# A convolution, Mamba and FFN network on one core: the FFN two steps later, and the scan's last column copied ahead of the product

## The chip, the cores and the metric

The kernel runs on one core of a Trainium2 chip. The metric is the device time of one execution in microseconds (us); the median of three runs before the change is 28348.76 us (28341.41 to 28352.17). A core has engines with queues of their own, each of which works strictly in order: TensorE (PE in the profile; PEld is its weight load), VectorE (DVE), ScalarE (ACT), GpSimd (POOL) and SyncE (SP, which here issues the DMAs). An instruction can wait for other engines through semaphores, and everything behind it on its engine waits too.

## The reference

Eight images of 64 channels and 128 x 128 pixels go through three parts: a front (a learned high-pass filter and norms), a bidirectional Mamba block of two layers, and a mix with an FFN. Cut to what the change touches:

```python
def selective_scan(u, dt, A, Bm, Cm, D, z):
    dt = jax.nn.softplus(dt)
    dA = jnp.exp(jnp.einsum('bdl,dn->bldn', dt, A))
    dBu = jnp.einsum('bdl,bnl,bdl->bldn', dt, Bm, u)
    ...
    _, hs = jax.lax.associative_scan(comb, (dA, dBu), axis=1)   # h = dA * h + dBu along l
    y = jnp.einsum('bldn,bnl->bdl', hs, Cm) + D[None, :, None] * u
    return y * jax.nn.silu(z)
...
g = conv2d(xn, ffn_in_w, pad=0)
g = conv2d(g, ffn_dw_w, groups=2 * HID, pad=1)
g1, g2 = jnp.split(g, 2, axis=1)
g = jax.nn.gelu(g1, approximate=False) * g2
return x + conv2d(g, ffn_out_w, pad=0)
```

A sequence has 16384 positions, 128 channels and 16 states per channel, and is scanned in both directions in each of the two layers.

## The kernel before

**The unit of work.** A sequence is cut into 16 chunks of T = 1024 positions. The 2048 pairs of channel and state are laid on 128 partitions in U = 16 rounds, so a chunk has 16 scan steps, an image has 4 x 16 chunks (1024 steps), and the eight images have 512 chunks and 8192 steps. All other work (front, mix and FFN of one image) is placed beside the Mamba steps of another.

**The order is written by hand.** `at(time, phase, fn)` puts a function into step `time`; within a step the phases run FEED, SCAN, MID, PROD, EXP, DECAY, REST. The functions are called in the order of (step, phase), and each engine's queue gets its instructions in that order. What an instruction waits for is worked out from the tiles that it reads and writes; two engines that touch the same PSUM bank are ordered one after the other, in the order of the program, reads against reads too.

**One scan step u** (class `Chunk`; `plan` places it with b as the chunk's first step):

- `drive` (L1216, GpSimd): for two steps at once `bu` = dt*u * B into SBUF, four buffers.
- `decay` (L1221, ScalarE, phase EXP of step b+u-2): `w` = exp(dt * A), 128 x 1024, into one of two PSUM tiles that take turns, so decay of u+2 writes over the tile of u.
- `scan` (L1231, VectorE, phase SCAN): h = w * h + bu, from the state column that the previous chunk left. If `on_pool(u)`, h goes to the SBUF tile `hs`; otherwise back into `w` in PSUM.
- `product` (L1257): h times C. On GpSimd one step later if `on_pool(u)`, otherwise on VectorE in phase PROD of the same step, from `w` into `hs`. `on_pool` is true for u = 0, 2, 6 modulo 8, but for the step after a gelu (`gelu_times`, L1052).
- `keep` (L1268, ScalarE): copies the last column of h, 128 x 1, into `state` for the next chunk. For a VectorE step its source is the PSUM tile `w`; it stands in phase PROD and, in the list of that phase, behind `product`.
- `collect` (L1271, TensorE): sums over the states into `y`.

On ScalarE's queue the copy of step u is followed by the decay of u+2 (EXP), then by what DECAY holds in that step (PSUM tiles copied out for conv, gate, dt, the norms and so on), then by REST.

**Functions with a table of their own.** ScalarE's exp and ln share one table; silu, softplus and gelu each load another and load the first back (`logs_and_exps`, L68). They stand in REST: `silu` at step 11 modulo 16 (silu of `xc`, in half of the chunks of the gate as well), `softplus` at step 2 modulo 16.

**The FFN** (class `Ffn`, images 0 to 6 beside the next image's Mamba; the last image's FFN runs alone at the end on another plan). Its 16 row blocks stand FFN_STEP = 24 steps apart, from step FFN_AT of the image. With a as a block's first step: windows loaded at a-4 and a-3, `conv` groups of four parts at a, a+6 and a+14, `first_out` at a+5, `gelus` at a+11 in REST, `rest_times` at a+13, `times` at a+19 and a+21, `load_x2` at a+16, `project` at a+21, `add` and `store` at a+23.

Of the kernel before, what the change touches and what calls it, by code (L numbers as in the profile page):

```python
# [36 lines left out]
FEED, SCAN, MID, PROD, EXP, DECAY, REST = range(7)  # L37

IMAGE = 4 * NT * U
FRONT_STEP, MIX_STEP, FFN_STEP = 24, 13, 24  # L40
FRONT_AT, MIX_AT, FFN_AT = 593, 990, 1202

SILU, SOFTPLUS, GELU = 11, 18, 11

# [11 lines left out]
def kernel(ctx: ExitStack, tc: tile.TileContext, a: dict, out: bass.AP):  # L56
# [6 lines left out]
    nc = tc.nc  # L63
# [124 lines left out]
    with tc.tile_pool(name="wspill", bufs=1) as fp, tc.tile_pool(name="wprep", bufs=2) as pp, \  # L188
            tc.tile_pool(name="wps", bufs=4, space=PSUM) as pps:
        with tc.manual_schedule():  # L190
# [161 lines left out]
            for l in range(DEPTH):  # L352
# [9 lines left out]
                for d in range(2):  # L362
                    cw, xdt, xbc, dtn, al, dp = dirs[2 * l + d]
                    taps = by_taps(inx2, cw, DI, KC)
                    for j in range(KC):
                        t = turned(taps[:, j, :], ident, P, DI)
                        at = j if d == 0 else KC - 1 - j
# [39 lines left out]
    def at(time, phase, fn, *args):  # L407
        steps.setdefault((time, phase), []).append((fn, args))
# [466 lines left out]
    class Ffn:  # L875
# [139 lines left out]
        def plan(self, a):  # L1015
            early = 12 if self.alone else 0
            at(a - 4 - early, REST, self.load, 0)
            at(a - 3 - early, REST, self.load, 1)

            if self.alone:  # L1020
                at(a - 6, REST, self.before_taps)
                at(a - 5, DECAY, self.before_taps_out)
                at(a - 5, REST, self.taps, 0)
                at(a - 2, REST, self.taps, 1)
                groups = ((0, 0, self.first_out, 2), (3, 1, self.times, 6))
                gelus, out = 3, 9
            else:
                groups = ((0, 0, self.first_out, 5), (6, 2, None, 0), (14, 1, self.times, 19))
                gelus, out = GELU, 21
            for t, g, end, to in groups:  # L1030
                for i in range(4):
                    at(a + t + (0 if self.alone else i), REST, self.conv, g, i)
                for h in range(2 if end else 0):
                    late = 0 if self.alone or end == self.first_out else 2 * h
                    at(a + to + late, MID if end == self.times else DECAY, end, h)
            at(a + gelus, REST, self.gelus)
            at(a + gelus + 2, MID, self.rest_times)
            at(a + out - 5, REST, self.load_x2)
            at(a + out, REST, self.project)
            at(a + out + 2, DECAY, self.add)  # L1040
            at(a + out + 2, REST, self.store)
# [18 lines left out]
    class Chunk:  # L1060
# [205 lines left out]
                nc.gpsimd.tensor_tensor(out[:, ::-1], hs[:, ::-1], c[:, ::-1], ALU.mult)  # L1266

        def keep(self, u):  # L1268
            nc.scalar.copy(self.column(u), self.last(self.hs.pop(u)))  # L1269

        def collect(self, k):  # L1271

# [72 lines left out]
        def plan(self):  # L1345
            b = self.t0 - 2 * U

            def feed(t, fn, *args):
                if self.beside_front:
                    at(t, FEED, fn, *args)  # L1350
                else:
                    at(t - 1, REST, fn, *args)

            at(b + (5 if self.i == NCH - 2 else 3), REST, self.load_hn)
            for h in range(2):
                feed(b + 7 + h, self.conv, h)
                at(b + 7 + h, DECAY, self.conv_out, h)
                if self.second:
                    feed(b + 9 + h, self.gate, h)
                    at(b + 9 + h, DECAY, self.gate_out, h)  # L1360
                feed(b + 14 + h, self.step, h)
                at(b + 14 + h, DECAY, self.step_out, h)
            at(b + SILU, REST, self.silu)
            at(b + SOFTPLUS, REST, self.softplus)
            if self.second:
                at(b + 13, REST, self.store_gate)
            b = self.t0
            feed(b - 16, self.bc)
            at(b - 16, DECAY, self.bc_out)
            at(b - 14, REST, self.store_bc)  # L1370
            at(b - 13, REST, self.store_dt)
            at(b - 11, FEED, self.dtx)
            at(b - 10, REST, self.store_du)
            j0 = self.pairs[0][0] // 2
            at(b - 10, REST, self.load_states, "bp", j0)
            at(b - 8, REST, self.load_channels, "dup", 0)
            at(b - 6, REST, self.load_channels, "dtp", 0)
            at(b - 5, REST, self.load_states, "bp", 1 - j0)
            at(b - 4, REST, self.load_states, "cp", j0)
            at(b - 3, REST, self.load_channels, "dup", 1)  # L1380
            at(b - 2, REST, self.load_channels, "dtp", 1)
            at(b - 1, REST, self.load_states, "cp", 1 - j0)
            for k in range(U // 2):
                at(b + 2 * k - 5, REST, self.drive, k)
                at(b + 2 * k + 3 + (k % 4 == 0), REST, self.collect, k)
            for u in range(U):
                at(b + u - 2, EXP, self.decay, u)
                at(b + u, SCAN, self.scan, u)
                at(b + u + self.on_pool(u), FEED if self.on_pool(u) else PROD, self.product, u)
            for u in range(U):  # L1390
                at(b + u + self.on_pool(u), EXP if self.on_pool(u) else PROD, self.keep, u)
            for h in range(2):
                if self.second:
                    at(b + 8 * h + 1, REST, self.load_yf, h)
                    at(b + 8 * h + 6, REST, self.add_yf)
                    at(b + 8 * h + 7, REST, self.load_gate, h)
                if self.second:
                    at(b + 8 * h + 11, MID, self.y_out, h)
                else:
                    at(b + 8 * h + 10, DECAY, self.y_out, h)  # L1400
                    at(b + 8 * h + 11, REST, self.store_y, h)
            if not self.second:
                return
            b += U
            n = self.norm
            at(b + 2, REST, self.load_h)
            feed(b + 5, self.project)
            at(b + 6, DECAY, self.residual)
            at(b + 6, DECAY, self.square)
            if self.l == 0:  # L1410
                at(b + 7, REST, self.store_h)
            feed(b + 12, lambda: n.means(mm_tile, self.sq))
            at(b + 13, DECAY, n.means_out)
            feed(b + 17, n.spread, mm_tile)
            at(b + 19, MID, self.normed)
            if self.l:
                at(b + 20, DECAY, self.weighted)
            at(b + 20, REST, self.store_hn)
# [10 lines left out]
    for b in range(B):  # L1429
        a, last = IMAGE * b, b == B - 1  # L1430
# [36 lines left out]
```

## Time and profile before

The profiled execution took 28355.4 us and its span is 28353.5 us, so 1.9 us lie around the span.

| engine | busy us | share of the span | instructions |
|---|---|---|---|
| VectorE | 26988.0 | 95% | 17438 |
| GpSimd | 26586.1 | 94% | 7980 |
| TensorE (matmul) | 23008.2 | 81% | 98188 |
| ScalarE | 18798.4 | 66% | 29139 |

The mean granted TensorE clock is 0.883 of full speed. In image 2 the stretch beside the FFN (7886 to 9178 us) takes 1292 us for 388 steps, the one beside the front (9187 to 10649 us) 1462 us for 424 steps, and the one beside the mix (10640 to 11330 us) 690 us for 208 steps. Read a row of the profile's groups as line, engine, operation, what is written from what, count, busy time and mean of one in ns, and then the idle time of the engine just ahead of these instructions with what ended most of it.

### The profile page before, as it was taken

The page shows a single profiled execution, that of the slowest core. Times are in us where ns is not written, and L with a number is a line of the kernel's source. Part 1 is how long each engine was busy: PE and PEld are TensorE (multiplying, and loading weights), DVE is VectorE, ACT ScalarE, POOL GpSimd, SP SyncE. Part 2 cuts the span into 40 slices and gives each one's busy share as a digit, 9 for nine tenths or more (in the row PEclk, how much of TensorE's full clock was granted, in tenths as well). Part 3 has the DMA queues.
Part 4 walks back from the last instruction along what each step waited for, and adds up shares of the span by engine and source line. Part 5 has one row for each costly group of instructions (what it writes and reads, how often), then busy time and mean ns, then how long its engine had stood idle before and what let it go on. Part 6 is the DMA issues. An engine that isn't in the chain of part 4 may idle for free. (4 is left out here: it accounts for less than half of the span.)

```text
span 28353.5 us, 311709 instructions
## 1 busy us (share of the span) xinstructions
PE 23008.2 (81%) x98188; PEld 7334.6 (26%) x98188; DVE 26988.0 (95%) x17438; ACT 18798.4 (66%) x29139; POOL 26586.1 (94%) x7980
## 2 busy tenths in 40 slices
PE   7666888878888788887888888887888878888679
PEld 3212322223222232222322223222222222222113
DVE  6999999999999999999999999999999999999997
ACT  4666666666666666666666666666666666666663
POOL 4999999999999999999999999999999999999994
PEclk7777889988899888988889888998888988899789
DMA  6777787777877678777787777777777777777675
GB/s 161 232 242 228 236 261 249 248 228 240 264 245 250 226 237 270 242 248 229 244 261 247 240 231 248 258 248 240 234 250 251 250 237 234 255 254 251 216 250 155
DMA packets 2611073, 6796.34 MB, mean 240 GB/s; under 512 B 433558, under 2 KB 739110, under 8 KB 2608390
## 3 DMA queue, kind: packets, MB, share of 16 engines
q1 hardware_dynamic: 2608534, 6776.25, 73.7%
q8 instruction: 776, 12.71, 0.2%
q14 instruction: 883, 7.23, 0.1%
q10 hardware_dynamic: 880, 0.14, 0.0%
HBM read 5543.05 MB, written 1265.19 MB: 240 GB/s over the span
## 5 line engine op out<-in xcount | busy, mean ns | idle before, releaser
L1218 POOL TENSOR_TENSOR bu<-dup,bp 128x2048 f32<-128x2048 f32 x4096 | 18594.4, 4548 | 52.2 <-DMA dup<-du_dram 26.1
L1226 ACT ACTIVATE w<-dtp,a_neg 128x1024 f32<-128x1024 f32 x8192 | 9163.6, 1119 | 1429.0 <-DVE hs L1247 601.6
L1262 DVE TENSOR_TENSOR hs<-w,cp 128x1024 f32<-128x1024 f32 x5232 | 6391.1, 1222 | 199.0 <-DMA cp<-bc_dram 46.6
L1247 DVE TENSOR_TENSOR_SCAN w<-w,state,bu 128x1024 f32<-128x1024 f32 x2651 | 6210.2, 2343 | 88.6 <-ACT w L1226 58.7
L1245 DVE TENSOR_TENSOR_SCAN w<-w,state,bu 128x1024 f32<-128x1024 f32 x2581 | 6048.2, 2343 | 121.8 <-ACT w L1226 105.0
L1284 PE MATMUL y<-hs,sel_y 128*32 128x512 f32 x32768 | 4944.7, 681 | 569.3 <-POOL hs L1266 445.5
L1269 ACT COPY state<-w 128x1 f32<-128x1 f32 x5232 | 828.0, 158 | 5178.4 <-DVE hs L1262 5119.6
L1264 POOL TENSOR_TENSOR hs<-hs,cp 128x1024 f32<-128x1024 f32 x1515 | 3593.5, 2372 | 428.4 <-DVE hs L1245 286.3
L1266 POOL TENSOR_TENSOR hs<-hs,cp 128x1024 f32<-128x1024 f32 x1445 | 3424.5, 2370 | 395.1 <-DVE hs L1247 351.8
L1245 DVE TENSOR_TENSOR_SCAN hs<-w,state,bu 128x1024 f32<-128x1024 f32 x1515 | 3550.6, 2344 | 151.9 <-ACT state L1269 79.3
L1247 DVE TENSOR_TENSOR_SCAN hs<-w,state,bu 128x1024 f32<-128x1024 f32 x1445 | 3384.5, 2342 | 78.0 <-ACT state L1269 43.0
L1093 PE MATMUL xp<-hn,wx 128*128 128x512 f32 x4096 | 2494.0, 740 | 1188.3 <-ACT xc L1099 567.8
L914 PE MATMUL fp<-fw,bgw 128*128 128x512 f32 (+1 forms) x5760 | 2118.5, 613 | 38.1 <-DMA fw<-xn_dram 34.0
L1135 PE MATMUL dp<-xc,wdt 128*128 128x512 f32 x2048 | 1331.6, 737 | 710.3 <-ACT dt L1142 392.1
L1284 PEld LDWEIGHTS y<-hs,sel_y 128*32 128x32 f32 x32768 | 720.2, 114 | 4256.0 <-issue 2609.4
L1277 PE MATMUL y<-xc,dskip 128*64 128x512 f32 x4096 | 1358.9, 748 | 415.9 <-ACT yv L1301 323.5
L1093 PEld LDWEIGHTS xp<-hn,wx 128*128 128x128 f32 x4096 | 845.8, 225 | 2679.6 <-issue 1047.3
L68 ACT ACT_TABLE_LOAD x1137 | 1458.8, 1283 | 20.8 <-PEq L1456 0.7
L1099 ACT ACTIVATE xc<-xp,cbias 128x512 f32<-128x512 f32 x1024 | 701.2, 685 | 1159.3 <-PE xp L1093 1156.5
L920 PE MATMUL fp<-fw,bgw 64*128 64x512 f32 (+1 forms) x5760 | 1379.1, 605 | 0.0
L607 PE MATMUL wb<-wt,sel_k 65*128 65x512 bf16 x1152 | 508.8, 442 | 1000.7 <-DVE t L611 994.3
L622 PE MATMUL acc<-t,ident 128*128 128x512 f32 x2160 | 1307.2, 693 | 0.0
(220 smaller groups left out, 26231.9 us busy)
## 6 DMA issues: line engine op xcount, KB each, us to landing
bp<-bc_dram SPq DMA_DIRECT2D x4096, 256.0 KB, 4.2
dup<-du_dram SPq DMA_DIRECT2D x4096, 256.0 KB, 5.2
dtp<-dt_dram SPq DMA_DIRECT2D x4096, 256.0 KB, 5.1
cp<-bc_dram SPq DMA_DIRECT2D x4096, 256.0 KB, 4.9
hn<-hn_dram SPq DMA_DIRECT2D x1024, 256.5 KB, 4.4
dt_dram<-dt SPq DMA_DIRECT2D x512, 512.0 KB, 3.0
du_dram<-du SPq DMA_DIRECT2D x512, 512.0 KB, 2.6
yf_dram<-yv SPq DMA_DIRECT2D x512, 256.0 KB, 3.1
```

The costliest lines, as they stand in the source:

```text
L68: nc.scalar.preload_act_table_set("natural_log_exp_and_others")
L914: nc.tensor.matmul(o, wpair[:, i, g, m], self.win[h][:, i : i + ROWS, 0:W], start=(i == 0), stop=False)
L920: nc.tensor.matmul(o, wlast[rows, i, g, m], self.win[h][rows, i : i + ROWS, lo : W + lo], start=False, stop=(i == 2),)
L1093: nc.tensor.matmul(self.xp[h], wx[:, self.l, self.d, i, :], self.hn2[:, s.start + 2 * i : s.stop + 2 * i], start=(i == 0), stop=(i == 1),)
L1218: nc.gpsimd.tensor_tensor(bu, self.dup[self.pairs[k][1]], self.over_pair("bp", k), ALU.mult)
L1226: nc.scalar.activation(w, self.dtp[gp][:, i, :], AF.Exp, scale=a_neg[:, self.l, self.d, g, j : j + 1])
L1245: nc.vector.tensor_tensor_scan(to, w, bu, s0, ALU.mult, ALU.add)
L1247: nc.vector.tensor_tensor_scan(to[:, ::-1], w[:, ::-1], bu[:, ::-1], s0, ALU.mult, ALU.add)
L1262: nc.vector.tensor_tensor(out, hs, c, ALU.mult)
L1264: nc.gpsimd.tensor_tensor(out, hs, c, ALU.mult)
L1266: nc.gpsimd.tensor_tensor(out[:, ::-1], hs[:, ::-1], c[:, ::-1], ALU.mult)
L1284: nc.tensor.matmul(self.y[lo : lo + 32, :], sel_y, hs[:, i, s], start=False, stop=(k % 4 == 3))
```

## The change

The FFN starts at step 1204 instead of 1202 of an image. Within a block `rest_times` stands three steps behind `gelus` instead of two, the two `times` both at a+20 instead of a+19 and a+21, and `project` at a+20 instead of a+21; `load_x2`, `add` and `store` hang on `project`. In steps of the image that is: loads, convs, `first_out` and `gelus` two later, `rest_times` three later, `times` at 1224 instead of 1221 and 1223, and `load_x2`, `project`, `add` and `store` one later. The gelu of a block then stands at step 15 or 7 modulo 16 instead of 13 or 5, so that the step whose product goes from GpSimd to VectorE is 0 modulo 8 instead of 6 modulo 8.

`keep` of a VectorE step moves from phase PROD to phase MID, so that it is called ahead of `product`; to that end it leaves the entry in `self.hs`.

```diff
-FRONT_AT, MIX_AT, FFN_AT = 593, 990, 1202
+FRONT_AT, MIX_AT, FFN_AT = 593, 990, 1204
...
-                groups = ((0, 0, self.first_out, 5), (6, 2, None, 0), (14, 1, self.times, 19))
-                gelus, out = GELU, 21
+                groups = ((0, 0, self.first_out, 5), (6, 2, None, 0), (14, 1, self.times, 20))
+                gelus, out = GELU, 20
...
                 for h in range(2 if end else 0):
-                    late = 0 if self.alone or end == self.first_out else 2 * h
-                    at(a + to + late, MID if end == self.times else DECAY, end, h)
+                    at(a + to, MID if end == self.times else DECAY, end, h)
             at(a + gelus, REST, self.gelus)
-            at(a + gelus + 2, MID, self.rest_times)
+            at(a + gelus + (2 if self.alone else 3), MID, self.rest_times)
...
         def keep(self, u):
-            nc.scalar.copy(self.column(u), self.last(self.hs.pop(u)))
+            nc.scalar.copy(self.column(u), self.last(self.hs[u]))
...
             for u in range(U):
-                at(b + u + self.on_pool(u), EXP if self.on_pool(u) else PROD, self.keep, u)
+                at(b + u + self.on_pool(u), EXP if self.on_pool(u) else MID, self.keep, u)
```

In the changed program the order of instructions within ScalarE's queue around the copy is the same (copy of u, decay of u+2). Other waits stand on them: the copy waits for the scan, the product waits for ScalarE (before, for its own engine's scan), and decay of u+2 waits for the product (before, for the copy).

## The prediction

> **What bounds it now.** I read the shares of the engines first (VectorE 95% of the span, GpSimd 94%, ScalarE 66%), then the costliest groups, the waits of ScalarE and of VectorE, and the timeline of both around one silu. The groups that one scan step is made of, and the table loads:
>
> ```profile
> L1226 ACT ACTIVATE w<-dtp,a_neg 128x1024 f32<-128x1024 f32 x8192 | 9163.6, 1119 | 1429.0 <-DVE hs L1247 601.6
> L1262 DVE TENSOR_TENSOR hs<-w,cp 128x1024 f32<-128x1024 f32 x5232 | 6391.1, 1222 | 199.0 <-DMA cp<-bc_dram 46.6
> L1247 DVE TENSOR_TENSOR_SCAN w<-w,state,bu 128x1024 f32<-128x1024 f32 x2651 | 6210.2, 2343 | 88.6 <-ACT w L1226 58.7
> L1269 ACT COPY state<-w 128x1 f32<-128x1 f32 x5232 | 828.0, 158 | 5178.4 <-DVE hs L1262 5119.6
> L68 ACT ACT_TABLE_LOAD x1137 | 1458.8, 1283 | 20.8 <-PEq L1456 0.7
> ```
>
> The product L1262 starts with almost no idle time (199 us over 5232), the copy L1269 sits idle ahead of itself for 5178 us: today the follower is ScalarE, and its waiting costs nothing. The waits of ScalarE (engine, line, waited for, us in total, times, longest):
>
> ```profile
> ACT state L1269 <- DVE hs L1262: 5119.6, 3159, 8.4
> ACT xc L1099 <- PE xp L1093: 1156.5, 728, 6.8
> ```
>
> Only 3159 of 5232 copies wait for the product. Nearly all the other 2073 start after the product has already ended: ScalarE comes to them late, and nobody minds. One such case, ScalarE and then VectorE (start, duration):
>
> ```profile
> 6001.04 0.16 ACT L1269 COPY state<-w 128x1 f32<-128x1 f32 x1 [1.37 <-DVE hs L1262]
> 6001.23 1.12 ACT L1226 ACTIVATE w<-dtp,a_neg 128x1024 f32<-128x1024 f32 x1
> ...
> 6002.89 1.28 ACT L1119 ACT_TABLE_LOAD   x1
> 6004.18 1.06 ACT L1119 ACTIVATE xc<-xc 128x1024 f32<-128x1024 f32 x1
> 6005.25 1.28 ACT L68 ACT_TABLE_LOAD   x1
> 6006.55 0.16 ACT L1269 COPY state<-w 128x1 f32<-128x1 f32 x1
> ```
>
> ```profile
> 6000.92 2.35 DVE L1247 TENSOR_TENSOR_SCAN w<-w,state,bu 128x1024 f32<-128x1024 f32 x1
> 6003.38 1.23 DVE L1262 TENSOR_TENSOR hs<-w,cp 128x1024 f32<-128x1024 f32 x1
> 6004.52 2.35 DVE L1247 TENSOR_TENSOR_SCAN w<-w,state,bu 128x1024 f32<-128x1024 f32 x1
> ```
>
> The product starts 0.11 us behind its scan, while ScalarE is in its silu; the copy of that step follows at 6006.55, 1.94 us after the product has ended.
>
> **The wait that the change turns round.** Copy and product read the same PSUM tile and stay ordered. Ahead of the product, the copy makes VectorE, the busiest engine, wait for ScalarE's in-order queue at 5232 places. In the case above the copy would end at 6006.71 at today's times, the product would start some 3.3 us late, and behind it stand the next scan on VectorE, the decay of u+2 on ScalarE, GpSimd's next product and `drive` (its four buffers are freed by scans), and the collects on TensorE.
>
> What replaces today's slack can be summed. At each VectorE product both engines now meet: decay of u+2 cannot start before the product's end, nor the next product before the next copy. From one product's end to the next scan's end VectorE takes 2.34 us plus what stands in MID; ScalarE must do a decay, 1.12, and a copy, 0.16, with about four handovers of 0.03 us (the median from product end to copy start is 0.034 us). So ScalarE has 2.34 - 1.12 - 0.16 - 0.12 = 0.94 us for all else, plus MID; what goes beyond is a stall of VectorE, and since both meet again, stalls add up with no carry-over. I went through the timelines of both engines from copy to copy (5232 stretches) and summed what each does besides scan, product, decay and copies:
>
> - **silu**, 510 stretches with one scan: ScalarE 4.34 us (silu and its two loads 3.65, with the gate 4.60, and some DECAY work), MID 0.10. Excess 4.34 - 0.10 - 0.94 = 3.30 us; 510 x 3.30 = **1682**.
> - **gelu**, 112 stretches with one scan: 4.58, MID 0; excess 3.64; **407**. Two steps later it meets the same neighbours: an odd step with a VectorE product, then a step taken off GpSimd.
> - **softplus**, 511 stretches with two scans (step 2 is GpSimd's, step 3 VectorE's): 4.46, MID 0.94. The decay released by the first scan comes ahead of softplus, so mostly one scan's slack counts: 511 x (4.46 - 0.94 - 0.94) = 1319 at most, 820 if all other work fits under the first scan. I take **1100**.
> - **the other 2448 stretches with two scans**: ScalarE 1.52, MID 0.44 on average. What exceeds the slack, summed stretch by stretch, is 208 if both scans' slack counts and 1146 if one does. I take **500**, nearer the low end, since DECAY work stands behind both decays. The 1650 with one scan hold 0.19 us and come to 9.
> - **ScalarE's waits for TensorE** within these stretches, xp above all, are 2398 us in the waits of ScalarE (all rows with PE as the one waited for that exceed 40 us). Bounds 0 (TensorE, 81% busy, catches up while VectorE stalls) and 2398; most fall where some slack is left. I take **1000**.
> - **the bare handover**, where ScalarE is free: 0.03 + 0.16 + 0.03 instead of the 0.04 to 0.11 us from scan to product now, some 0.15 us. 3565 products have nothing between scan and product, about 750 of them stand behind a table load: 2800 x 0.15 = **420** (300 to 800). With a 0.67 us MID operation between, it is hidden.
> - **given back**: VectorE idles 28353.5 - 26988.0 = 1365.5 us now. Of it 417 us are scans waiting for ScalarE and GpSimd, which both gain time; about 585 us are waits for TensorE. I take **-600** (0 to -1000).
>
> A rule speaks for still more. The Trainium skill, "ScalarE: Activation LUTs", section "What ACT_TABLE_LOAD costs", puts a switch of tables at 1283 ns of load plus about 1380 ns of drain. The trace has the load but not the drain: the load at 6002.89 lasts 1.28 us, and the function behind it starts at 6004.18. By the page a silu would hold ScalarE for some 2.7 us longer, and 1136 of them would add about 3100 us (an estimate from that page); the rows decide, and the sum goes without it.
>
> **The FFN's other moves** I cost at nothing, within 150 us. The same 112 blocks issue the same instructions: per block two window loads of two DMAs, two loads and two stores on SyncE's queue one or two steps later, ahead of uses four or five steps off; the convs and the projection move on TensorE with the tiles they read; one product per gelu leaves GpSimd as before. 224 `times` of 0.68 us go from steps with a VectorE product, where they would hide a copy, into one step with GpSimd's: at most 224 x 0.68 = 152 us of cover, and in the next stretch they give it back. A gain by the wider gap between gelu and silu is bounded by all that VectorE waits for decays today: 105.0 + 68.9 + 58.7 + 8.0 = 241 us.
>
> The sum, on the profiled span: 28353.5 + 1682 + 407 + 1100 + 500 + 9 + 1000 + 420 - 600 = 32871.5. The profiled execution, 28355.4 us, is 6.6 us above the median of the runs, so I say **32850 us**, 15.9% slower. All low ends together give 28353.5 + 1682 + 407 + 820 + 208 + 300 - 1000 = 30770, all high ends 28353.5 + 1682 + 407 + 1319 + 1146 + 9 + 2398 + 800 = 36115.
>
> **Rivals.** *Only the handover* (5%): ScalarE, 66% busy, gets ahead everywhere once it may copy early, and the product pays 0.15 us alone: 28350 + 5232 x 0.15 = 29130. For it: the copy and its handover leave the path product - copy - decay. Against it: the silu block is longer than a scan, whoever starts it early.
> *Everything late stays late* (9%): each product starts, at today's times, only after the instruction ahead of its copy and the copy itself. Summed over all 5232 that is 6930 us: 35280. It counts a backlog at several products in a row, where one stall already clears it; for it speaks that TensorE's waits stay whole.
> *Faster* (3%): product and decay are what matters, the 0.16 us copy no longer stands between them, and the gelu no longer follows silu within two steps. All waits of VectorE's scans for ScalarE and GpSimd vanish: 28350 - 417 = 27930. It decides if the product waits for the copy less than 417 / 5232 = 0.08 us on average, which is less than the copy's own 0.16 us; it needs the product not to be held at all. That the change doesn't do what it says (the product runs on beside the copy) ends here too. Against it: in the changed program the product does carry a wait on ScalarE.
>
> **How the numbers follow.** The forecast has 83% with 31300 to 34400, which leaves out the corners where all unknowns fall on one side; the range is the same, since the rivals outside hold 17%. Faster by over 0.2%, about what a measurement here can tell from no change: 2%. Within 0.2%: 1%, where gain and handover cancel. Slower: 97%.
>
> **What would show it.** The idle time ahead of the product's line, 199 us now, must be the largest of VectorE's, 4000 us or more, released by ScalarE's copy; longest behind silu, gelu and softplus, near 3 us each. The copy must wait for the scan, and the decay for the product. VectorE's share must fall to about 26988 / 32850 = 82%, GpSimd's to 81%, with their busy times unchanged. I am wrong if that idle time stays under 1000 us, or if the stalls stand at TensorE's products rather than behind table loads.

## The result, and the profile after

| | median us | runs |
|---|---|---|
| before, same chip | 28350.25 | 28341.41 to 28352.17 |
| changed | 32947.04 | 32945.54 to 32959.34 |

The ratio is 1.1623, with a 95% interval of 1.161 to 1.1637: 16% slower, and 97 us from the forecast. The profiled execution has a span of 32957.3 us.

The shares of the engines and the groups of one scan step in the changed kernel (its `keep` is L1268, its product L1261, its decay L1225, its scans L1244 and L1246):

```profile
PE 24459.4 (74%) x98188; PEld 7776.7 (24%) x98188; DVE 26987.9 (82%) x17438; ACT 18832.8 (57%) x29139; POOL 26624.7 (81%) x7980
...
L1225 ACT ACTIVATE w<-dtp,a_neg 128x1024 f32<-128x1024 f32 x8192 | 9160.9, 1118 | 8801.2 <-DVE hs L1261 6924.1
L1261 DVE TENSOR_TENSOR hs<-w,cp 128x1024 f32<-128x1024 f32 x5232 | 6400.5, 1223 | 5484.1 <-ACT state L1268 5483.8
L1246 DVE TENSOR_TENSOR_SCAN w<-w,state,bu 128x1024 f32<-128x1024 f32 x2651 | 6211.2, 2343 | 0.0
...
L1268 ACT COPY state<-w 128x1 f32<-128x1 f32 x5232 | 829.9, 159 | 2648.7 <-DVE w L1246 1422.8
```

VectorE does the same work (26987.9 us against 26988.0) in a longer span. The idle time ahead of its product went from 199.0 to 5484.1 us, all of it released by ScalarE's copy. The copy now waits for the scan, and the wait for the product has moved on to the decay (6924 us). The scans that followed the product, which had waited 78 to 152 us per group, have almost no idle time left (8 us in all four groups). The sums close: 5484.1 - 199.0 = 5285 us more ahead of the product; VectorE's other idle time went from 28353.5 - 26988.0 - 199.0 = 1166.5 to 32957.3 - 26987.9 - 5484.1 = 485.3, so 681 us were given back; 5285 - 681 = 4604, which is the difference of the spans (4603.8).

One silu in the changed kernel, ScalarE and then VectorE (start, duration, and in brackets the idle time before and its releaser):

```profile
6933.16 1.12 ACT L1225 ACTIVATE w<-dtp,a_neg 128x1024 f32<-128x1024 f32 x1 [1.29 <-DVE hs L1261]
...
6934.96 1.28 ACT L1118 ACT_TABLE_LOAD   x1
6936.25 1.06 ACT L1118 ACTIVATE xc<-xc 128x1024 f32<-128x1024 f32 x1
6937.33 1.28 ACT L68 ACT_TABLE_LOAD   x1
6938.62 0.16 ACT L1268 COPY state<-w 128x1 f32<-128x1 f32 x1
6940.07 1.12 ACT L1225 ACTIVATE w<-dtp,a_neg 128x1024 f32<-128x1024 f32 x1 [1.29 <-DVE hs L1261]
```

```profile
6933.05 2.35 DVE L1246 TENSOR_TENSOR_SCAN w<-w,state,bu 128x1024 f32<-128x1024 f32 x1
6938.81 1.23 DVE L1261 TENSOR_TENSOR hs<-w,cp 128x1024 f32<-128x1024 f32 x1 [3.42 <-ACT state L1268]
6939.95 2.35 DVE L1246 TENSOR_TENSOR_SCAN w<-w,state,bu 128x1024 f32<-128x1024 f32 x1
6942.53 1.23 DVE L1261 TENSOR_TENSOR hs<-w,cp 128x1024 f32<-128x1024 f32 x1 [0.23 <-ACT state L1268]
```

The scan ends at 6935.40, the product starts at 6938.81, 0.03 us after the copy behind the second table load. One step later ScalarE is on time, and the bare handover costs 0.23 us. The 1.29 us in front of the decay are ScalarE's new idle time: copy done, it waits for the product.

The idle time ahead of the product, summed by what ScalarE did since the last copy (from the timelines of both engines, stretch by stretch as in the prediction):

| stretch | count | before us | changed us | mean, changed |
|---|---|---|---|---|
| silu | 511 | 28 | 1751 | 3.43 |
| softplus | 511 | 7 | 1204 | 2.36 |
| gelu | 112 | 7 | 568 | 5.07 |
| other, one scan | 1650 | 85 | 297 | 0.18 |
| other, two scans | 2448 | 72 | 1664 | 0.68 |

### The profile page after: what moved, and what is told of

Its sections match the earlier page's. It is cut to its first block, busy times and chain, and to the rows that moved or that the text cites. A ratio compares the mean times of both kernels' runs of the same rounds, so it can differ in the third digit from the quotient of the medians.

```text
span 32957.3 us, 307213 instructions
## 1 busy us (share of the span) xinstructions
PE 24459.4 (74%) x98188; PEld 7776.7 (24%) x98188; DVE 26987.9 (82%) x17438; ACT 18832.8 (57%) x29139; POOL 26624.7 (81%) x7980
## 5 line engine op out<-in xcount | busy, mean ns | idle before, releaser
L1225 ACT ACTIVATE w<-dtp,a_neg 128x1024 f32<-128x1024 f32 x8192 | 9160.9, 1118 | 8801.2 <-DVE hs L1261 6924.1
L1261 DVE TENSOR_TENSOR hs<-w,cp 128x1024 f32<-128x1024 f32 x5232 | 6400.5, 1223 | 5484.1 <-ACT state L1268 5483.8
L1246 DVE TENSOR_TENSOR_SCAN w<-w,state,bu 128x1024 f32<-128x1024 f32 x2651 | 6211.2, 2343 | 0.0
L1244 DVE TENSOR_TENSOR_SCAN w<-w,state,bu 128x1024 f32<-128x1024 f32 x2581 | 6046.5, 2343 | 0.6 <-ACT w L1225 0.6
L1283 PE MATMUL y<-hs,sel_y 128*32 128x512 f32 x32768 | 5291.5, 700 | 120.4 <-DVE hs L1261 120.1
L1092 PE MATMUL xp<-hn,wx 128*128 128x512 f32 x4096 | 2561.3, 758 | 1521.4 <-ACT xc L1098 850.8
L1244 DVE TENSOR_TENSOR_SCAN hs<-w,state,bu 128x1024 f32<-128x1024 f32 x1515 | 3549.5, 2343 | 5.2 <-ACT w L1225 3.4
L1246 DVE TENSOR_TENSOR_SCAN hs<-w,state,bu 128x1024 f32<-128x1024 f32 x1445 | 3383.6, 2342 | 2.1
L1134 PE MATMUL dp<-xc,wdt 128*128 128x512 f32 x2048 | 1499.5, 822 | 2054.4 <-ACT dt L1141 1001.0
L914 PE MATMUL fp<-fw,bgw 128*128 128x512 f32 (+1 forms) x5760 | 2440.0, 667 | 283.2 <-DVE gt L976 251.6
L1268 ACT COPY state<-w 128x1 f32<-128x1 f32 x5232 | 829.9, 159 | 2648.7 <-DVE w L1246 1422.8
L502 PE MATMUL rb<-ident,r 128*64 128x128 f32 x12288 | 1032.2, 321 | 867.4 <-ACT bc L1160 336.2
L920 PE MATMUL fp<-fw,bgw 64*128 64x512 f32 (+1 forms) x5760 | 1487.2, 637 | 0.0
```

Source lines behind the costliest of these rows:

```text
L914: nc.tensor.matmul(o, wpair[:, i, g, m], self.win[h][:, i : i + ROWS, 0:W], start=(i == 0), stop=False)
L920: nc.tensor.matmul(o, wlast[rows, i, g, m], self.win[h][rows, i : i + ROWS, lo : W + lo], start=False, stop=(i == 2),)
L1092: nc.tensor.matmul(self.xp[h], wx[:, self.l, self.d, i, :], self.hn2[:, s.start + 2 * i : s.stop + 2 * i], start=(i == 0), stop=(i == 1),)
L1134: nc.tensor.matmul(self.dp[h], wdt[:, self.l, self.d, :], self.xc[:, halves[h]], start=True, stop=True)
L1225: nc.scalar.activation(w, self.dtp[gp][:, i, :], AF.Exp, scale=a_neg[:, self.l, self.d, g, j : j + 1])
L1244: nc.vector.tensor_tensor_scan(to, w, bu, s0, ALU.mult, ALU.add)
```

## The experiments

Each time stands beside runs of the kernel before on the same chip (three chips; median 28384 to 28391 us there, 34 to 41 us above the 28350 us beside the changed kernel). So ratios are compared, or the distance of each run from the kernel before on its own chip, which for the changed kernel is 32947.0 - 28350.3 = 4597 us.

**e1, the copy alone.** The `keep` part of the diff, the FFN as before.

```diff
-                at(b + u + self.on_pool(u), EXP if self.on_pool(u) else PROD, self.keep, u)
+                at(b + u + self.on_pool(u), EXP if self.on_pool(u) else MID, self.keep, u)
```

> The copy moved ahead of the product, the FFN as before. Theory (the copy's wait is the whole loss, the FFN's moves cost nothing): 32750 to 33150 us. Rival (the FFN's moves make part of the loss, since the stall behind a gelu came out at 5.1 us instead of 3.6 and both products of a block now stand in one step): 32500 us or less.

Measured: 32582.90 us, ratio 1.1478 (1.1459 to 1.1498). It lies between the two, nearer the rival's 32500. The copy makes 4199 us of loss, and the FFN's moves add some 400 us on top of it (4597 - 4199 = 398), which is not nothing. VectorE's longest wait in e1 (us in total, times, longest):

```profile
DVE hs L1262 <- ACT state L1269: 5138.3, 4020, 6.2
```

Against the changed kernel's 5484 us this is 346 us less. Of these, 177 us stand behind gelu, 118 in the other stretches with two scans and 51 in those with one; why the stretches without gelu grew too was not tried.

**e2, the FFN alone.** The FFN's part of the diff, `keep` back in PROD.

> The FFN moved, the copy behind the product as before. Theory: within 150 us of before, at most 241 us faster (VectorE's waits for decays): 28100 to 28500 us. Rival (the FFN's moves cost by themselves): 28600 us or more.

Measured: 28620.38 us, ratio 1.0082 (1.0067 to 1.0097), 236 us slower: outside the theory's range and at the rival's bound (28350 x 1.0082 = 28583 us). The FFN's moves do cost by themselves. By step, the stretch beside the FFN went from 1301.9 to 1336.3 us for 392 steps (mean over images 1 to 6); for the seven images with an FFN beside the next one that is 7 x 34.4 = 241 us; beside front and mix nothing changed (1443.2 and 1443.0; 707.8 and 708.5). Who waited for whom on VectorE in e2 (us in total, times, longest):

```profile
DVE hs L1246 <- ACT w L1225: 220.2, 92, 5.2
...
DVE w L1246 <- ACT w L1225: 100.5, 122, 3.2
```

Before, the first of these rows was 8.0 us. The four rows of scans that wait for a decay sum to 220.2 + 100.5 + 87.7 + 71.3 = 480 us, against 241 before. One such wait in e2's timeline, ScalarE and then VectorE:

```profile
8289.48 0.69 ACT L1141 ACTIVATE dt<-dp,dtb 128x512 f32<-128x512 f32 x1 [2.11 <-PE dp L1134]
8290.19 1.28 ACT L969 ACT_TABLE_LOAD   x1
...
8293.14 1.28 ACT L68 ACT_TABLE_LOAD   x1
...
8294.62 1.12 ACT L1225 ACTIVATE w<-dtp,a_neg 128x1024 f32<-128x1024 f32 x1
```

```profile
8291.91 1.22 DVE L1261 TENSOR_TENSOR hs<-w,cp 128x1024 f32<-128x1024 f32 x1
8295.83 2.35 DVE L1246 TENSOR_TENSOR_SCAN hs<-w,state,bu 128x1024 f32<-128x1024 f32 x1 [2.69 <-ACT w L1225]
```

At step 15 ScalarE's queue holds the copy of `dt` out of PSUM (`step_out`) ahead of gelu. It waits 2.11 us for TensorE, gelu starts that much later, the decay behind it too, and a scan stands still for 2.69 us. At step 7 the same place is held by `conv_out`. Over all 112 blocks of e2, ScalarE waited 158 us for TensorE at these copies, and each copy takes another 0.68 us. At the old steps, 13 and 5, 70 blocks of the kernel before have no copy out of PSUM between the decay and gelu but those of the state, and 42 have the norm's `means_out` (0.47 us, at step 13), ahead of which no wait for TensorE shows.

**e3, the copy behind the product where a table load has just run.** From the changed kernel:

```diff
+                late = (self.t0 + u) % U in (3, 12) or self.t0 + u - 1 in gelu_times
-                at(b + u + self.on_pool(u), EXP if self.on_pool(u) else MID, self.keep, u)
+                at(b + u + self.on_pool(u), EXP if self.on_pool(u) else PROD if late else MID, self.keep, u)
```

> The changed kernel, but in the steps right behind silu, softplus and gelu (steps 12 and 3 modulo 16, and the step after a gelu) the copy stands behind the product as before. Theory (the stalls are ScalarE's blocks with table loads): the 3515 us of idle time ahead of those products go, and 0.2 to 1.0 us per block comes back at the next product, where ScalarE is still late: 29650 to 30600 us. Rival (the loss is the bare handover and TensorE's waits, spread over all products): 31500 us or more.

Measured: 30457.67 us, ratio 1.073 (1.0714 to 1.0746), 2073 us above the kernel before, so 4597 - 2073 = 2524 us of the loss are gone, as the theory has it. The idle time ahead of the blocks' products fell from 3523 to 54 us; that of the other stretches with one scan rose from 297 to 1325, since ScalarE is still late at the next product: 1028 us, 0.9 us for each of the 1134 blocks. The product's row in e3:

```profile
L1261 DVE TENSOR_TENSOR hs<-w,cp 128x1024 f32<-128x1024 f32 x5232 | 6400.7, 1223 | 2960.4 <-ACT state L1268 2895.3
```

**e4, exp for softplus in the changed kernel**, and **e7, the same in the kernel before**:

```diff
-            nc.scalar.activation(dt, dt, AF.Softplus)
-            logs_and_exps()
+            nc.scalar.activation(dt, dt, AF.Exp)
```

> The changed kernel with exp in the place of softplus, which needs no other table, so that two loads of 1.28 us per chunk are left out (the output is not softplus's). Theory: the stall behind softplus, 1204 us in all, shrinks to the bare handover of 0.2 us: 31700 to 32100 us. Rival (a block is made up for later, or TensorE sets the time): less than 400 us faster, 32550 us or more.

> The kernel before with exp in the place of softplus, as in e4 (the output is not softplus's): some 1300 us of ScalarE's work left out. Theory (a late copy is free as long as nobody waits for it): within 120 us of before, against 1175 us in the changed kernel. Rival (softplus's block holds VectorE in the kernel before too): 400 us faster or more.

Measured: e4 31772.16 us, ratio 1.1193 (1.1176 to 1.1209), 3388 us above the kernel before, so 4597 - 3388 = 1209 us of the loss are gone; e7 28350.19 us, ratio 0.9986 (0.9977 to 0.9995), 41 us less than before. The same two table loads per chunk, some 1350 us of ScalarE's busy time, are worth some 1200 us in one kernel and 41 in the other. For this one function, that is the turned wait measured by itself. The stall at softplus's place fell from 1204 to 133 us, and the product's row in e4 is:

```profile
L1260 DVE TENSOR_TENSOR hs<-w,cp 128x1024 f32<-128x1024 f32 x5232 | 6399.1, 1223 | 4281.1 <-ACT state L1267 4278.9
```

**e5 and e6, the two halves of the FFN's moves.** The copy behind the product in both; e5 has the new places within a block with the FFN at 1202, e6 the old places with the FFN at 1204.

> The copy behind the product as before, the FFN at step 1202 as before (gelu at steps 13 and 5 modulo 16), but within a block the new places (gelu's product three steps behind, both products and the projection at a+20). Theory (the FFN's 236 us come from where gelu stands: at 15 and 7 it stands between ScalarE's copies out of PSUM for dt and for the conv, which wait for TensorE): within 100 us of before. Rival (both products in one step, or the projection right behind them, cost it): at least 150 us slower than before.

> The copy behind the product as before, the FFN at step 1204 (gelu at steps 15 and 7), within a block the old places. Theory (gelu's neighbours): 180 to 300 us slower than before. Rival (the places within a block): within 100 us of before.

Measured: e5 28430.43 us, ratio 1.0013 (1.0004 to 1.0021), 40 us; e6 28707.43 us, ratio 1.0111 (1.0097 to 1.0125), 317 us, a little above the range given. So the shift by two steps makes the loss. The new places within a block win back some 80 us of it at 1204. Two waits on VectorE in e6:

```profile
DVE ga L979 <- PE fp L920: 210.6, 88, 6.8
...
DVE hs L1247 <- ACT w L1226: 135.1, 71, 3.8
```

The first is `times` waiting for TensorE, 47.6 us in the kernel before and 30.5 in e2. The four rows of scans that wait for a decay sum to 348 us in e6, more than before (241) but less than in e2 (480). So with the old places the late gelu is a part of the 317 us, and `times` makes another. At 1202 the new places cost 40 us; from what was not tried.

**e8, gelu ahead of the step's copies.** As e2, with gelu in another phase:

```diff
-            at(a + gelus, REST, self.gelus)
+            at(a + gelus, REST if self.alone else EXP, self.gelus)
```

> As e2 (the FFN moved as in the change, the copy behind the product), but gelu stands in phase EXP, behind the decay and ahead of the step's copies out of PSUM, so that it doesn't wait for TensorE's products in front of it. Theory (gelu is late because ScalarE's queue holds a copy that waits for TensorE ahead of it): most of the 236 us come back, 28350 to 28480 us. Rival (the wider or narrower distance to silu and softplus, or the plan within a block, decides): 28550 us or more.

Measured: 28460.17 us, ratio 1.0025 (1.0016 to 1.0035), 71 us slower than before, as the theory has it: 165 of the 236 us came back, with gelu in the same step as in e2 and so with its distances to softplus and silu nearly the same. The row of 220.2 us in e2 is here:

```profile
DVE hs L1246 <- ACT w L1225: 52.1, 92, 4.8
```

The four rows of scans that wait for a decay sum to 355 us, against 480 in e2 and 241 before. So scans still wait longer for ScalarE than before; what makes the 71 us that are left was not tried.

**e9, all three functions ahead of their step's copies, in the kernel before.** `silu`, `softplus` and `gelus` in EXP.

> The kernel before with silu, softplus and gelu each in phase EXP ahead of their step's copies out of PSUM. If blocks that start earlier help wherever a copy ahead of them waits for TensorE: 50 to 250 us faster than before (all waits of scans for ScalarE in the kernel before are some 395 us). If the copies behind them come too late for TensorE instead: the same or slower.

Measured: 28358.85 us, ratio 0.999 (0.9981 to 0.9999), 30 us faster than before: less than was hoped, and at the edge of what can be told, but the only version here that does the whole computation and is below both kernels.

## Why the prediction was right, and where it was not

*The turned wait.* Shown. The product now stands behind ScalarE's queue at 5232 places; e1 puts the copy alone at 1.1478, and e4 against e7 shows, for softplus, that a late ScalarE was nearly free before (41 us) and is paid for now (some 1200 us).

*The sum by stretches.* Silu 1682 forecast, 1751 measured; softplus 1100, 1204 (820 to 1319 held). The stretches without a load, forecast as 500 + 9 for work, 1000 for TensorE and 420 for the handover, 1929 in all, hold 297 + 1664 = 1961. Of these 4098 products, 3425 idle by 0.3 us or less and make 578 us, mostly 0.23 us each: that is the bare handover, above the 420 us taken but within its 300 to 800. The other 673 make 1384 us. In 525 of their stretches ScalarE had waited for TensorE, and the smaller of that wait and the stall, summed over them, is 1238 us: at most so much is TensorE's. How much of it is, and how much is ScalarE's own work, was not separated by a run, so the good sum does not show that each of its terms was right. The upper bound of 2398 us for TensorE had also counted waits before the first of these stretches and after the last; between them the trace before has 2069.

*Given back:* 600 forecast, 681 measured.

*No carry-over.* This held: the product next after a block idles 0.18 us on average in the changed kernel. Every VectorE product had become a meeting point. Where e3 took the meeting away behind the blocks, 0.9 us per block were carried to the next product.

*The FFN's moves at nothing, within 150 us:* wrong. They cost 236 us alone and some 400 us on top of the copy. The step that failed is the sentence that two steps later gelu meets the same neighbours. It looked at VectorE's side alone, a product before and after. On ScalarE's queue the neighbours changed: `step_out` at steps 14 and 15 and `bc_out` at 0, `conv_out` at 7 and 8, and gelu came to stand behind copies at which ScalarE waits for TensorE, 158 us in e2. With gelu ahead of them (e8), 165 of the 236 us came back. The gelu term carries the same error: 407 forecast, 568 measured, while e1 with gelu at the old steps has 391. The bound on a gain by the wider gap was not tested, for the sign was the other one.

*The total* was met to 97 us partly by luck, since two misses have opposite signs. With the FFN's moves at nothing, the forecast of 32850 stands for the copy alone, which measured 28350 x 1.1478 = 32540, 310 us less; the FFN's moves then added some 400. In e1 the stalls came out lower than summed (5138.3 - 199.0 = 4939 us against 5118) and more was given back (671 us against 600).

*The rivals.* "Only the handover" falls with the table: 3523 of 5484 us stand behind blocks. "Everything late stays late" falls with the product next after a block, which waits 0.18 us on average. "Faster" falls with the result, and with e1 for the copy alone.

*The drain of the Trainium skill* ("ScalarE: Activation LUTs", "What ACT_TABLE_LOAD costs"), about 1380 ns for each switch of tables, is not seen after the change either: the load at 6934.96 ends at 6936.24 and silu starts at 6936.25. Over all 2282 loads of either kernel, the median time is 0.02 us from the instruction ahead to the load and 0.01 us from the load to the next. The sum without the drain was the one that held.

## What to carry to other kernels

Before a wait between two engines is turned round, ask which of the two is allowed to be late. Here an in-order queue with blocks of 3.6 to 4.6 us in it cost next to nothing as a follower (41 us for softplus) and 2.4 to 5.1 us per block as a leader, though the engine was busy for only 66% of the time. When a long block is moved, look at what its own queue holds in front of it and behind it: here two steps put gelu behind copies that wait for another engine and cost 236 us, and taking it out from behind them gave 165 us back.

## What the runs showed of the hardware

TensorE's mean granted clock was lower in the runs in which it was busy for a smaller share: 0.883 of full speed at a busy share of 81% before, 0.836 at 74% in the changed kernel, with 0.842 at 74% (e1), 0.85 at 76% (e4) and 0.859 at 78% (e3) between. The same 98188 matmuls are recorded as 24459.4 us of busy time instead of 23008.2. Why the clock was lower, and what of the changed kernel's waits for TensorE comes from that, was not tried.
